# Additive-tanh attention on one Trainium2 core: weighing the 32-row query terms of the next block later in the tanh stretch

## The chip, the cores and the metric

The kernel runs on one core of a Trainium2 chip. The core has a matrix engine (PE, with its weight loads shown as PEld), a vector engine (DVE), a scalar engine for activation functions (ACT), a general engine (POOL) and a queue engine that issues transfers (SP). The metric is the device time of one execution in microseconds (us). The program is launched once and computes the whole model, so the time holds much more than the part that is changed here.

## The reference

The model has an image part (layer 0: projections, a small convolution, a selective scan in four directions) and a token part (layer 1: attention, then a recurrent layer). Only the attention bears on the change. It works on 4 batches of 4096 tokens (64 x 64) with 128 channels, and has 32 hidden units:

```python
t = _to_tokens(x)                                  # 4 x 4096 x 128
t = t + _L1_attn_ref(_ln_t(t), Wt, Wx, bh, Wa, ba)

def _L1_attn_ref(x, Wt, Wx, bh, Wa, ba):
    q = jnp.einsum('bld,ud->blu', x, Wt)           # 32 units for each query
    k = jnp.einsum('bld,ud->blu', x, Wx)           # 32 units for each key
    beta = jnp.tanh(q[:, :, None, :] + k[:, None, :, :] + bh)
    alpha = jnp.einsum('bsju,u->bsj', beta, Wa[:, 0]) + ba[0]
    alpha = jnp.tanh(alpha)
    alpha = jax.nn.softmax(alpha, axis=-1)
    return jnp.einsum('bsj,bjd->bsd', alpha, x)
```

For each pair of a query and a key a sum of 32 weighted tanh terms is formed, then a tanh of that sum, then a softmax over the 4096 keys of a query, and the weights are applied to the normalised tokens. The inner tanh over 4 x 4096 x 4096 x 32 elements is what the kernel avoids.

## The kernel before

Three parts run one after the other: `_layer0`, then the attention `_rational` (from line 1242 on), then the recurrent layer `_chunked`. Only `_rational` changes. Inside it the instructions go to each engine's queue in the order in which the Python program writes them; no scheduler moves them. An instruction waits for the ones it depends on, and everything behind it in the same engine's queue waits with it. Tiles come from pools with a fixed number of buffers, so a new tile also waits until the oldest one has been read.

**The mathematics.** tanh(q + k) is a ratio of expressions in exp(q) and exp(k), and a group of several such terms is one fraction whose numerator and denominator are sums of products of one factor of the query with one factor of the key. The factors of the queries are kept in `E` (128 rows x 2 sides x 512 queries), those of the keys in `F` (128 rows x 2 sides x 4096 keys). A matrix product of some rows of `F` with the same rows of `E` gives the denominators (tile `pd`, function `lower`), and a product with the weighted rows `cE` gives the numerators (tile `pn`, function `upper`). `cE` is `E` times one constant per row, formed by `weigh` (L1379): two DVE instructions, one for each side, of 128 x 512 elements. All products of these two functions have the line L1393 in the profile.

The rows are cut into three units. Unit A uses side 0 in two terms of 64 rows. Units B1 and B2 use side 1, each in two terms of 32 rows. `cE`'s side 0 is read only by `upper` of A, its side 1 only by `upper` of B1 and of B2.

**Blocks and key tiles.** There are 32 blocks: 4 batches, in each 8 blocks of 512 queries. Each block goes over 32 key tiles (`jt`) of 128 keys, and each key tile over the three units. In the steady loop one unit is: two products into `pd` (PE), Ln of it on ACT (L1524), Exp of the negative on ACT (L1527), so that these two form the reciprocal, two multiplications with the numerators on DVE (`times`, L1414), and for B1 and B2 an addition to the sum of unit A on POOL (L1533). `whole` (L1518) on DVE then adds the two halves of the tile's ratio and stores the argument of the outer tanh for 128 keys x 512 queries in `A[:, jt, :]`. In the loop, PE writes the `pd` of a unit two steps ahead and its `pn` one step ahead. The pools have 2 buffers for `pd`, 3 for `pn`, 1 for the product `ct`, 4 and 5 for the ratios `ra` and `rb`, and 1 for `cE`.

Single steps lie between the units of the loop as well, held in the table `between`: the queries of the next block, the transposes of the next batch, the layer norm of the next batch's tokens (`norm_within`, not in the last batch), and the end of the block before (`closing`). Its last step adds the result to the residual tile `xr` on POOL (L1462).

**The block change.** After the last key tile, ACT needs another function table and has the tanh and the exponential of the whole block to do (L1583, L1584), in four parts of 4, 8, 8 and 12 key tiles (`PARTS`). During this stretch, the "tanh stretch", ACT can form no reciprocals, so the next block's first key tile is done by DVE alone, in the function `direct`: for each half of a unit a reciprocal (L1424) and a multiplication with the numerator (L1425). The function `ahead` writes it in four steps, one behind each part of the tanh: step 0 forms the `pd` of A and B1, `upper` of A and `direct` of A; step 1 the `pd` of B2, `upper` and `direct` of B1 and the POOL addition L1574; step 2 the next key tile's `pd` of A, then `upper` and `direct` of B2 and the addition L1578; step 3 another `pd`. Between the steps PE forms `weighted` (L1557), the product of the finished weights with the tokens `xT`, for the parts up to key tile 20; the other 12 key tiles' products lie in the next block's loop. `direct` has an argument `then`, called once behind the first half of its unit; step 0 uses it for the last `whole` of the old block.

Before the change, DVE's order at a block change is therefore: the `times` of the old block's last units, `cE` side 0, `cE` side 1, then for unit A reciprocal, product, `whole`, reciprocal, product, then the same pairs for B1 and B2. PE's order is: the `pd` of A and B1, `upper` A, `weighted` of 0 to 3, the `pd` of B2, `upper` B1, `weighted` of 4 to 11, the `pd` of the next A, `upper` B2, `weighted` of 12 to 19, the `pd` of the next B2, and then the loop.

Where the batch changes (three times: behind blocks 7, 15 and 23) the block is "turned": the factors `F` of all keys of the new batch are formed first (`all_keys`, L1342 to L1351, with 16 maxima on DVE), ahead of step 0 and behind `weigh`.

## Time and profile before

| what | us |
|---|---|
| median of 3 runs | 10629.57 |
| the runs | 10622.62 to 10634.68 |
| profiled execution, its own time | 10622.87 |
| span of the profile in that execution | 10621.1 |
| PE, DVE, ACT, POOL busy, whole span | 9213.9, 9043.7, 9094.5, 8609.3 |
| the same from 3750 to 10400 us, a stretch of 6650 us that is all attention | 6209.2, 5517.2, 6530.7, 5074.8 |
| mean granted clock of PE | 0.942 of full speed |

An execution on one core is profiled by the hardware; the page that is made of it gives the busy time of each engine, the span in 40 slices, and groups of instructions with count, busy time, mean time of one (ns), and the idle time of the engine ahead of them with what ended it. A line such as `x1986 | 2443.0, 1230 | 26.9 <-PE pd L1393 24.6` reads: 1986 instructions, 2443.0 us busy, 1230 ns each; ahead of them the engine stood idle for 26.9 us, of which 24.6 ended when PE had finished a product into `pd` of line 1393. `32*128 32x512 f32` at a product are the rows of its weights and the columns, then the rows and columns of what is moved through. "PEclk" and "granted clock" are the TensorE clock that the throttle granted, as a share of full speed. In the timeline, the first figure is the start in us from the start of the span, the second the time until the last of the group's instructions ended, and in square brackets stands the idle time ahead of it with what ended it. Line numbers are those of the kernel before.

### The profile page before, as it was taken

To read this page: it belongs to the slowest core of one execution; us is meant where nothing else is said; L and a number is where in the kernel's file an instruction comes from. 1 tells how busy PE (TensorE), PEld (TensorE's weight loads), DVE (VectorE), ACT (ScalarE), POOL (GpSimd) and SP (SyncE) were. 2 spreads that over 40 slices of the span, in tenths; PEclk is the share of its full clock that TensorE was granted. 3 is DMA by queue.
4 is the path that set the end of the run, shared out by engine and by line. 5 is a ranking of instruction groups with operands and counts; after the bars stand their busy time and mean duration, and the time that the engine had idled before them with its cause. 6 is when DMAs were issued, how large, how long until landed. Compare 5 with 4: busy or idle time off the path is not lost.

```text
span 10621.1 us, 110120 instructions
## 1 busy us (share of the span) xinstructions
PE 9213.9 (87%) x35452; PEld 3226.5 (30%) x35452; DVE 9043.7 (85%) x10031; ACT 9094.5 (86%) x10279; POOL 8609.3 (81%) x3686
## 2 busy tenths in 40 slices
PE   7787787787777799999999999999999999999997
PEld 2121221222211233333333333333333333333334
DVE  7999999999999788888888888888888888888882
ACT  4566666766766799999999999999999999999995
POOL 7999899999999777788678778877888777767773
PEclk8898898898888999999999999999999999999998
DMA  6889889888888200000000000000000000000001
GB/s 150 200 191 213 189 193 212 194 197 209 198 199 203 71 4 4 4 4 7 4 4 4 7 4 4 7 4 4 4 7 4 4 3 5 3 3 3 5 2 66
DMA packets 228573, 739.50 MB, mean 70 GB/s; under 512 B 41536, under 2 KB 42368, under 8 KB 226448
## 3 DMA queue, kind: packets, MB, share of 16 engines
q1 hardware_dynamic: 224576, 730.76, 29.2%
q8 instruction: 280, 4.59, 0.2%
q14 instruction: 309, 2.53, 0.1%
q10 hardware_dynamic: 3408, 1.63, 0.1%
HBM read 609.15 MB, written 118.88 MB: 69 GB/s over the span
## 4 chain that ended last, share of the span: by engine, by line
PE 35%; ACT 21%; DVE 5%; issue 5%; POOL 1%; DMA 0%; DVEq 0%; POOLq 0%; ACTq 0%; SPq 0%
PE pd L1393 16%; PE pn L1393 10%; PE ct L1557 6%; ACT rb L1527 6%; ACT rb L1524 6%; ACT ra L1524 2%; ACT A L1583 2%; DVE rb L1414 2%; ACT ra L1527 2%; ACT A L1584 1%; DVE ra L1424 1%; PE vy L1758 1%; POOL ra L1533 0%; DVE cE L1379 0%; ACT E L1300 0%
## 5 line engine op out<-in xcount | busy, mean ns | idle before, releaser
L1533 POOL TENSOR_TENSOR ra<-ra,rb 128x1024 f32<-128x1024 f32 x1986 | 5000.9, 2519 | 813.0 <-ACT rb L1527 446.5
L1393 PE MATMUL pn<-cE,F 32*128 32x512 f32 (+1 forms) x12288 | 4602.5, 643 | 88.3 <-DVE rb L1414 78.0
L1393 PE MATMUL pd<-E,F 32*128 32x512 f32 (+1 forms) x12288 | 4037.8, 650 | 342.9 <-ACT ra L1524 239.8
L1414 DVE TENSOR_TENSOR rb<-rb,pn 128x512 f32<-128x512 f32 x3972 | 2543.4, 682 | 582.4 <-PE pn L1393 576.8
L1527 ACT ACTIVATE rb<-rb 128x1024 f32<-128x1024 f32 x1986 | 2513.6, 1270 | 0.0
L1524 ACT ACTIVATE rb<-pd 128x1024 f32<-128x1024 f32 x1986 | 2443.0, 1230 | 26.9 <-PE pd L1393 24.6
L786 POOL TENSOR_TENSOR dBu<-dtdu,bbcc 128x1024 f32<-128x1024 f32 x1024 | 2391.4, 2365 | 88.8 <-DMA dtdu<-dd 58.2
L1393 PEld LDWEIGHTS pd<-E,F 32*128 32x128 f32 (+1 forms) x12288 | 1209.9, 186 | 2257.2 <-ACT ra L1524 972.1
L1393 PEld LDWEIGHTS pn<-cE,F 32*128 32x128 f32 (+1 forms) x12288 | 1420.9, 186 | 1317.3 <-DVE rb L1414 647.0
L1414 DVE TENSOR_TENSOR ra<-ra,pn 128x512 f32<-128x512 f32 x1986 | 1356.1, 686 | 384.8 <-PE pn L1393 287.4
L826 PE MATMUL py<-h,gather 128*32 128x512 f32 x4096 | 1190.6, 677 | 391.7 <-POOL h L812 372.9
L1527 ACT ACTIVATE ra<-ra 128x1024 f32<-128x1024 f32 x993 | 1258.0, 1267 | 0.0
L1524 ACT ACTIVATE ra<-pd 128x1024 f32<-128x1024 f32 x993 | 1210.4, 1219 | 52.6 <-PE pd L1393 43.7
L781 ACT ACTIVATE pa<-dtdu,a_neg 128x1024 f32<-128x1024 f32 x1024 | 1143.6, 1117 | 34.7 <-DMA dtdu<-dd 11.2
L802 DVE TENSOR_TENSOR_SCAN pa<-pa,carry,dBu 128x1024 f32<-128x1024 f32 x480 | 1125.4, 2345 | 32.3 <-ACT pa L781 22.9
L1557 PE MATMUL ct<-A,xT 128*128 128x512 f32 x2048 | 1046.4, 639 | 10.5 <-ACT A L1584 10.5
L812 POOL TENSOR_TENSOR h<-h,bbcc 128x1024 f32<-128x1024 f32 x381 | 899.3, 2360 | 121.8 <-ACT carry L810 104.9
L810 ACT COPY carry<-pa 128x1 f32<-128x1 f32 x643 | 103.0, 160 | 883.9 <-DVE h L809 883.3
L809 DVE TENSOR_TENSOR h<-pa,bbcc 128x1024 f32<-128x1024 f32 x643 | 787.7, 1225 | 61.7 <-PE py L826 1.7
L1518 DVE TENSOR_TENSOR A<-ra 128x512 f32<-128x512 f32 x993 | 753.9, 759 | 35.9 <-POOL ra L1533 31.6
L802 DVE TENSOR_TENSOR_SCAN h<-pa,carry,dBu 128x1024 f32<-128x1024 f32 x288 | 673.2, 2341 | 21.3 <-PE py L826 10.6
L826 PEld LDWEIGHTS py<-h,gather 128*32 128x32 f32 x4096 | 221.8, 116 | 1255.9 <-issue 529.0
(306 smaller groups left out, 8282.2 us busy)
## 6 DMA issues: line engine op xcount, KB each, us to landing
bbcc<-bcd SPq DMA_DIRECT2D x1024, 256.0 KB, 7.7
dtdu<-ddd SPq DMA_DIRECT2D x1008, 256.0 KB, 7.8
ddd<-dd SPq DMA_DIRECT2D x63, 1024.0 KB, 5.1
src<-src SPq DMA_DIRECT2D x60, 512.0 KB, 9.7
xs<-in_x_dram SPq DMA_DIRECT2D x32, 256.0 KB, 7.3
src<-xs SPq DMA_DIRECT2D x16, 512.0 KB, 6.2
bcd<-bc SPq DMA_DIRECT2D x64, 128.0 KB, 1.9
src<-xsT SPq DMA_DIRECT2D x16, 512.0 KB, 5.4
```

Source lines behind the costliest of these rows:

```text
L781: nc.scalar.activation(dA, its[m].DT[r][:, 0, :], AF.Exp, scale=a)
L786: nc.gpsimd.tensor_tensor(dBu, its[m].DT[r][:, 1, :], its[m].BC[q][:, 0, :], ALU.mult)
L802: nc.vector.tensor_tensor_scan(to[:, step], dA[:, step], live.pop(("dBu", u))[:, step], 0.0 if m % nch == 0 else its[m - 1].carry[:, col : ...
L809: nc.vector.tensor_tensor(h, dA, cc, ALU.mult)
L812: nc.gpsimd.tensor_tensor(h, h, cc, ALU.mult)
L826: nc.tensor.matmul(it.y[to, c], gather, live["h", v][:, c], start=False, stop=(q == QS - 1))
L1393: nc.tensor.matmul(ps[a], F[lo:hi, i, jt * P : (jt + 1) * P], side[lo:hi, i, :], start=True, stop=True)
L1414: nc.vector.tensor_tensor(r[:, a, :], r[:, a, :], ns[a], ALU.mult)
L1524: nc.scalar.activation(r, D.pop(i), AF.Ln, scale=LOWER)
L1527: nc.scalar.activation(r, r, AF.Exp, scale=-1.0)
L1533: nc.gpsimd.tensor_tensor(R[at, 0], R[at, 0], R.pop((at, p)), ALU.add)
L1557: nc.tensor.matmul(ct, xT[:, jt, :], A[:, jt, :], start=(jt == 0), stop=(jt == JT - 1))
```

## The change

`weigh` no longer does its two multiplications itself. It makes the tile `cE` and returns it with a function `side(i)` that does one of them. At the kernel's start both sides are still done at once. At each of the 31 block changes side 0 is done where both were done before, and side 1 is done inside `direct` of the next block's unit A: behind the second half's product with the numerator, the place that the argument `then` now names as a pair (behind the first half the old block's last `whole`, as before; behind the second half side 1). The first step that reads side 1 is `upper` of B1, in `ahead(1)`.

DVE's order at a block change becomes: `cE` side 0, reciprocal, product, `whole`, reciprocal, product (unit A), `cE` side 1, then the pairs of B1 and B2. The order on PE, ACT, POOL and SP is as before. The lines behind L1379 move by one to five in the changed kernel.

```diff
--- before.py
+++ after.py
@@ -1375,9 +1375,11 @@
 
     def weigh(E):
         cE = one.tile([P, 2, QB], F32, name="cE")
-        for i in range(2):
+
+        def side(i):
             nc.vector.tensor_scalar(cE[:, i, :], E[:, i, :], c_n[:, i : i + 1], None, ALU.mult)
-        return cE
+
+        return cE, side
 
     groups = {
         "A": (0, ((0, 64), (64, 128))),
@@ -1424,8 +1426,7 @@
             nc.vector.reciprocal(r[:, a, :], d[:, a, :])
             nc.vector.scalar_tensor_tensor(r[:, a, :], r[:, a, :], 1.0 / LOWER, ns[a], ALU.mult, ALU.mult)
             if then is not None:
-                then()
-                then = None
+                then[a]()
         return r
 
     def order(jt):
@@ -1479,7 +1480,9 @@
     for steps in [keys(F, xn, 0, pn, i) for i in range(2)] + [queries(E, xn, 0, i) for i in range(2)]:
         for go in steps:
             go()
-    cE = weigh(E)
+    cE, side = weigh(E)
+    for i in range(2):
+        side(i)
     start = 0
     first = lower("A", F, 0, E), lower("B1", F, 0, E)
     between = {}
@@ -1550,7 +1553,9 @@
             assert not between
 
             if more:
-                E, cE = E_next, weigh(E_next)
+                E = E_next
+                cE, side = weigh(E)
+                side(0)
             ct = pw()
 
             def weighted(jt, ct=ct, xT=xT):
@@ -1567,7 +1572,7 @@
                     return
                 if step == 0:
                     held["A"], held["B1"] = lower("A", F, 0, E), lower("B1", F, 0, E)
-                    held["A"] = direct(held["A"], upper("A", F, 0, cE), "A", lambda: whole(JT - 1))
+                    held["A"] = direct(held["A"], upper("A", F, 0, cE), "A", (lambda: whole(JT - 1), lambda side=side: side(1)))
                 elif step == 1:
                     held["B2"] = lower("B2", F, 0, E)
                     held["B1"] = direct(held["B1"], upper("B1", F, 0, cE), "B1")
```

## Prediction

> **What bounds the kernel now.** I read the page first: from slice 14 on, ACT, PE and DVE are all near full, so the page alone cannot say which one sets the pace of the attention. The stretches of single blocks say it. A block here is the time from one table load of L1583 to the next.

> ```profile
> core 0: us, PE busy (x) PEld busy (x) DVE busy (x) ACT busy (x) POOL busy (x), PEclk, DMA share, GB/s
> 8016.00:8224.00 208.00, 195.69 (x844) 71.22 (x844) 174.85 (x243) 207.15 (x202) 162.02 (x66) 0.98 0.01 5
> 9082.00:9294.00 212.00, 194.66 (x842) 72.14 (x840) 174.09 (x241) 206.22 (x199) 162.49 (x66) 0.97 0.01 3
> ```

> ACT is busy 207.15 of 208.00 us in a short block and hardly less in a long one: ACT paces a block, and a block is long by the time ACT stands idle. Listed by their starts, 15 of the 31 block changes stand before no ACT idle at all (start to start 208.1 us); four wait 0.34 to 0.81 us; nine wait 2.29 to 2.46 us (210.5 to 211.8 us); three, where the batch changes, last 228 us. The waits of ACT over the attention give the whole sum:

> ```profile
> ACT ra L1524 <- PE pd L1393: 43.5, 37, 2.7
> ACT rb L1524 <- PE pd L1393: 24.6, 15, 2.5
> ```

> The second line holds the waits at block changes: 24.6 us is the ceiling of what a shorter change can give. The first line is mostly a stall inside the blocks, which returns below. Next, the timelines of two changes, a clean one (load at 8016.29) and a waiting one (load at 9082.91):

> ```profile
> 8018.58 3.89 DVE L1379 TENSOR_SCALAR cE<-E,consts 128x512 f32<-128x512 f32 x2
> 8022.39 3.35 DVE L1424 RECIPROCAL ra<-pd 128x512 f32<-128x512 f32 x1
> 8023.80 5.13 PE L1557 MATMUL ct<-A,xT 128*128 128x512 f32 x8
> 8030.45 0.70 PE L1393 MATMUL pd<-E,F 32*128 32x512 f32 x2 [1.53 <-DVE ra L1424]
> 8040.70 7.13 PE L1557 MATMUL ct<-A,xT 128*128 128x512 f32 x16
> 8049.00 1.02 ACT L1524 ACTIVATE rb<-pd 128x1024 f32<-128x1024 f32 x1
> ...
> 9088.20 3.70 PE L1557 MATMUL ct<-A,xT 128*128 128x512 f32 x8 [0.40 <-ACT A L1584]
> 9097.11 1.22 PE L1393 MATMUL pd<-E,F 32*128 32x512 f32 x2 [5.21 <-DVE ra L1424]
> 9099.13 8.50 PE L1557 MATMUL ct<-A,xT 128*128 128x512 f32 x16
> 9117.97 1.02 ACT L1524 ACTIVATE rb<-pd 128x1024 f32<-128x1024 f32 x1 [2.33 <-PE pd L1393]
> ```

> The reader should follow one chain: DVE cE, reciprocals of A, the release of pd to PE, then PE without a hole to the pd that ACT's second Ln (L1524) needs. In the second change the same 16 products take 8.50 us instead of 7.13 and the first 32-row product 1.22 instead of 0.70: PE runs at half clock. The granted clock in fine stretches confirms it, 0.50 from 9095.08 to 9101.89; in the clean change the half clock fell earlier, 8016.47 to 8026.70, under the tanh, where nobody waits. All such stretches are multiples of 3.41 us, on one grid.

> **What moves.** Per block change one instruction: cE's side 1 goes from ahead of the first reciprocal to behind the second product of unit A. No DMA, no ACT or PE instruction moves; DVE alone is reordered, and no queue is passed.

> At the old place side 1 is dear, because POOL is still adding: the lone pair at 3611.6 us took 0.48 us each, and behind POOL's last adds the pair takes 3.89 us; of it the second is 2.58 and holds DVE 2.5. At the new place, 12 us after the load, POOL is idle (it stands 17.2 us before L1574), so I take 0.48. DVE's chain gains 2.5 at its head and is 2.0 shorter behind side 1.

> [...]

> Who else waits for side 1? PE's upper of B1, and behind it in PE's order all `weighted` of 4 to 12. In a clean change upper A ends at 8023.9 (half clock), so product A0 can't start before that: 8023.9, 0.6, whole 0.6, reciprocal 3.45, product 0.6, side 1 0.5 gives 8029.6, against 8030.45 for PE's release now. PE finishes its `weighted` at 8028.93. So it comes 0.9 us earlier, not 2.5, for all that follows to 8048.9. ACT does not follow: it had no idle there, and its Tanh, Exp and table load end at 8048.0 whatever PE does. Gain of a clean change: 0.

> The four waits of 0.34 to 0.81 us fall to 0, since 0.9 to 1.7 exceeds them: 3 x 0.81 + 0.34 = 2.8 us. In the nine waiting changes PE ends `weighted` at 9091.9 and the release moves from 9097.1 to 9094.6, with side 1 at 9095.7. The hole shrinks from 5.2 to 2.7, yet the stretch 9091.67 to 9095.06 stays nearly empty, so the half clock still begins at 9095.1. Upper B1 (2.0 at half clock), then 4.1 us of half-rate products and 4.9 at full rate end at 9106.9 instead of 9107.55: a gain of 0.65 of 2.33.

> **What it costs.** PE now reaches the start of the next loop earlier, but its third pd comes free only when ACT has read the first (8048.0 + 1.02). PE's hole before it grows from 0.18 to 1.1 us, in the grid stretch 8047.17 to 8050.58, which held 4.0 (all products weighted by rows, one 128-row pass as 1; a full stretch holds 7.8). The 0.9 us of `weighted` that leaves is 0.9 / 0.441 = 2 passes, so 2.0 to 2.8 stay. Counted over the attention, every stretch followed by half clock held 2.9 or less, and every other one 3.1 or more. So I expect half clock in 8050.6 to 8054.0. There the unit-A products (0.53 a step, 1.0 at half) come 1.6 us late where Ln had 0.35 slack: ACT loses 1.0 to 1.6, say 1.4; two stretches would make 2.1.

> How little a hole need be is seen inside the blocks, where every block has the same 2.15 us hole (POOL's xr add delays whole):

> ```profile
> 8170.96 0.69 PE L1393 MATMUL pn<-cE,F 64*128 64x512 f32 x1 [2.15 <-DVE rb L1414]
> ...
> 9027.70 1.22 PE L1393 MATMUL pn<-cE,F 64*128 64x512 f32 x1 [2.15 <-DVE rb L1414]
> ```

> One hole, two outcomes: a boundary of the grid cuts the first in two. [...]

> **Sum** on the profiled execution (span 10621.1, its own time 10622.87, 6.70 under the median 10629.57):
> - Clean changes: 15 x 1.4, but only for phases where the stretch holds hole and loop start (2.6 of 3.41): +16.
> - Waiting changes: -2.8, and two of the first three batches x 0.65 = -1.3.
> - Last batch: seven blocks of 211.6 us x 0.65 = -4.6, say -5.
> - Batch changes: the first reciprocal there follows the key reductions, so taking side 1 from the front saves nothing; upper B1 now waits for it, one product, side 1: ACT's wait 0.36 becomes 1.7. 3 x 1.3 = +4.
> - The hole inside: blocks now sit at 208.1, close to 61 x 3.41 = 208.2, so the phase stays where the hole is cut. Longer blocks lose that. 0.65 of 3.41 us of phase is safe, so 81% of 23 blocks against 5 now, at 0.5 to 1.9, mean 1.0: 0 to 14, I take half, +7.

> Together +18: 10640.9, and 10648 at the median. A measurement of this kernel tells 0.2% (21 us) from no change.

> **Rivals.**
> [...]
> - *Slower: lasting collision of POOL and DVE.* Place: `whole` (L1518), 2.83 instead of 0.69 when a POOL add starts first. The last full block (load 10141.1) shows it after a half-clock event: waits of 2.1 and 2.7 us more, 216.7 us. Price about 2 us in each block; from half the blocks on it decides: 18 + 16 x 2 = +50, 10680.
> - *It does nothing*: excluded on DVE (2.5 us goes), possible for ACT, which then shows only phase drift, within 9 us.

> **Chances.** Forecast case 0.50 (its parts run from +0 to +35, so 0.28 within 0.2%, 0.22 slower); first rival 0.28 (0.13 within, 0.15 faster); collision 0.19, slower; nothing 0.03. So faster 0.15, same 0.44, slower 0.41. Range: from the cheap end of the first rival, 10608, to past the collision, 10688; its own range for the forecast case is 10630 to 10665.

> **What would show it.** Right: second cE near 0.48 us; PE's hole before `lower` B2 gone in clean changes; granted clock 0.50 about 34 us after a load; ACT idle about 38 us after it; fewer 208.1 blocks. Wrong: block starts still 208.1 apart and L1524's 24.6 us fallen to a few.

## The result

The changed kernel takes 10677.57 us (median of 5 runs, 10666.58 to 10683.64) against 10629.57 us (median of 5, 10622.62 to 10641.11): a ratio of 1.0044 with a 95% interval of 1.0032 to 1.0057, 48 us more. The profiled executions stand 60.7 us apart (spans 10681.8 and 10621.1). Of that, 56 us lie in the 31 blocks from one table load of the tanh to the next (6609.4 us together against 6553.4).

What the change does to DVE is what was forecast. This is a clean change (the half clock of the tanh stretch, 7642.19 to 7652.43 us, falls where nobody waits for it) of the new kernel, with the load at 7641.84 us, from the timelines of DVE, PE and ACT:

```profile
7644.13 1.40 DVE L1380 TENSOR_SCALAR cE<-E,consts 128x512 f32<-128x512 f32 x1
7645.45 3.34 DVE L1426 RECIPROCAL ra<-pd 128x512 f32<-128x512 f32 x1
...
7654.55 0.48 DVE L1380 TENSOR_SCALAR cE<-E,consts 128x512 f32<-128x512 f32 x1
...
7674.63 1.13 PE L1395 MATMUL pd<-E,F 32*128 32x512 f32 x4 [1.12 <-ACT ra L1527]
...
7678.98 1.02 ACT L1527 ACTIVATE ra<-pd 128x1024 f32<-128x1024 f32 x1 [0.68 <-PE pn L1395]
```

Side 1 is done in 0.48 us instead of 2.58. The first reciprocal starts 3.61 us after the load, 2.5 us earlier than before. PE comes early to the loop and stands for 1.12 us there. Then follows the half clock (0.50 from 7676.35 us), and ACT waits 0.68 us. The stretch with PE's hole, the stretch of the half clock behind it, and the two kinds of block that the new kernel has most of, by windows:

```profile
core 0: us, PE busy (x) PEld busy (x) DVE busy (x) ACT busy (x) POOL busy (x), PEclk, DMA share, GB/s
7672.93:7676.35 3.42, 2.30 (x12) 0.72 (x10) 0.69 (x1) 3.41 (x5) 0.83 (x1) 1.00 0.00 0
7676.35:7679.75 3.40, 3.40 (x12) 0.98 (x12) 1.38 (x2) 2.72 (x4) 0.00 (x0) 0.50 0.02 5
...
7641.84:7850.72 208.88, 197.63 (x845) 71.16 (x845) 173.13 (x243) 207.35 (x201) 162.56 (x66) 0.97 0.01 4
...
4437.56:4649.18 211.62, 196.96 (x845) 71.72 (x845) 172.88 (x243) 207.46 (x201) 161.79 (x66) 0.98 0.01 4
```

ACT's work is the same in both (207.4 us), so a block is long by what ACT waits, as before. But no block of the new kernel lasts 208.1 us, where 13 did; twelve of the 31 last 211.5 to 211.8 us, where six did. 211.63 us are 62 stretches of the clock's grid (62 x 3.4133; 945 such stretches lie between the starts of the new kernel's half clocks at 4450.73 and 7676.32 us). Ten blocks of the first two batches stand on that value one behind the other (1 to 6 and 11 to 14, counted by their table loads from 0). ACT's waits over the attention:

```profile
ACT ra L1527 <- PE pd L1395: 62.4, 54, 2.7
ACT rb L1527 <- PE pd L1395: 41.7, 22, 3.2
ACT E L1300 <- DVE top L1297: 18.9, 8, 2.4
```

The first was 43.5 and the second 24.6; the third, the exponentials of the next queries waiting for DVE, is not among the first five of before. Sorted by their place in the block (my sums over the rows of ACT's timeline), the waits at the loop start rose by 18 us (26.2 to 44.6), those at and just behind the stall inside the block by 25 us (44.6 to 70.0), the others in the loop by 11 us, and those in the tanh stretch fell by 3.5 us. These sums mix two opposite movements. The 21 ordinary blocks of the first three batches lost 44 of the 56 us: there the waits at the loop start rose by 22 us (7.6 to 29.9), and those at the stall, 120 us further on, by 13 us (17.8 to 31.0). In the seven blocks of the last batch, which lost 7 us, the waits at the loop start fell by 11 us and those at the stall by 6 us, while 17 us of waits that the kernel before did not have came just behind the stall.

**Why ten blocks hold at 62 stretches.** Call a block's phase the time from the last line of the 3.41 us grid to its table load. At phase 0.48 the new kernel's block runs like this (the block from 4437.56 us, from the timelines of PE and ACT and by windows): the half clock from 4450.73 to 4457.55 makes ACT wait 2.01 us at the loop start; the hole inside the block then lies almost wholly in the stretch from 4590.67 to 4594.08, and the next stretch has the half clock too.

```profile
4449.24 1.13 PE L1395 MATMUL pd<-E,F 32*128 32x512 f32 x4 [2.68 <-DVE ra L1426]
...
4472.31 1.02 ACT L1527 ACTIVATE rb<-pd 128x1024 f32<-128x1024 f32 x1 [2.01 <-PE pd L1395]
```

```profile
4450.73:4457.55 6.82, 6.82 (x11) 2.27 (x8) 6.72 (x3) 6.79 (x3) 0.00 (x0) 0.50 0.00 0
4590.67:4594.08 3.41, 1.49 (x8) 0.55 (x4) 3.25 (x2) 3.41 (x6) 2.44 (x2) 1.00 0.53 154
4594.09:4597.50 3.41, 3.19 (x12) 1.02 (x12) 2.04 (x4) 1.82 (x4) 2.35 (x1) 0.50 0.00 0
```

The columns of the windows are as above; the clock is the third from the end. ACT's timeline behind the hole:

```profile
4596.45 1.02 ACT L1527 ACTIVATE ra<-pd 128x1024 f32<-128x1024 f32 x1 [1.59 <-PE pd L1395]
```

The wait of 1.59 us stands where the clean block from 7641.84 us has 0.66 (at 7798.48). With 0.37 more behind it, the block comes to 211.62 us, and the next one starts at the same phase.

The order of before meets the same phase in one block of a run shown below (e7, load at 8028.71 us, phase 0.43; this batch's code is that of before). Its wait at the loop start is longer, 2.83 us, and so its hole ends 157.52 us after the load instead of 156.75. A line of the grid cuts it in two, and the clock stays full (windows, then ACT's timeline at the loop start and behind the hole):

```profile
8028.71:8239.65 210.94, 193.80 (x845) 70.99 (x845) 174.87 (x243) 207.26 (x201) 162.05 (x66) 0.98 0.01 5
8041.94:8048.76 6.82, 5.88 (x13) 2.32 (x14) 6.61 (x5) 6.79 (x3) 0.00 (x0) 0.50 0.00 0
8181.89:8185.30 3.41, 2.18 (x12) 0.59 (x4) 2.55 (x1) 3.41 (x6) 3.13 (x2) 1.00 0.44 152
8185.30:8188.71 3.41, 2.48 (x15) 0.94 (x18) 2.89 (x6) 2.75 (x5) 1.77 (x1) 1.00 0.01 5
```

```profile
8064.28 1.02 ACT L1530 ACTIVATE rb<-pd 128x1024 f32<-128x1024 f32 x1 [2.83 <-PE pd L1394]
...
8187.43 1.02 ACT L1530 ACTIVATE ra<-pd 128x1024 f32<-128x1024 f32 x1 [0.66 <-PE pd L1394]
```

210.94 us is 0.69 short of 62 stretches, so the phase moves back by 0.69 us, and the next block lasts 208.10 us. So the shorter wait of the new order is the dearer one. This rests on one block of the old order; blocks of e5, with a little more work on ACT, wait 2.8 us at the same phases and also keep the full clock behind the hole (e5, 4436.76 us: a wait of 2.82 us, then 1.00 in the three stretches from 4590.4 to 4600.6).

### The profile page after: what moved, and what is told of

Same layout as the page of the kernel before. It is cut to its first block, busy times and chain, and to the rows that moved or that the text cites. A ratio compares the mean times of both kernels' runs of the same rounds, so it can differ in the third digit from the quotient of the medians.

```text
span 10681.8 us, 110120 instructions
## 1 busy us (share of the span) xinstructions
PE 9252.4 (87%) x35452; PEld 3232.9 (30%) x35452; DVE 9006.2 (84%) x10031; ACT 9099.9 (85%) x10279; POOL 8605.3 (81%) x3686
## 4 chain that ended last, share of the span: by engine, by line
PE 38%; ACT 18%; DVE 5%; issue 4%; POOL 1%; DMA 0%; DVEq 0%; ACTq 0%; SPq 0%; POOLq 0%
PE pd L1395 17%; PE pn L1395 11%; PE ct L1562 7%; ACT rb L1530 6%; ACT rb L1527 5%; ACT ra L1527 2%; DVE rb L1416 2%; ACT ra L1530 2%; ACT A L1588 1%; DVE ra L1426 1%; ACT A L1589 1%; PE vy L1763 1%; POOL ra L1536 1%; DVE A L1521 0%; ACT E L1300 0%
## 5 line engine op out<-in xcount | busy, mean ns | idle before, releaser
L1521 DVE TENSOR_TENSOR A<-ra 128x512 f32<-128x512 f32 x993 | 779.0, 785 | 39.7 <-POOL ra L1536 35.1
```

## The experiments

The first four ran with the theory that PE's early arrival is the cause. A new order that is dear by itself would be dear in any kernel; so most of the later ones put the same edit into both orders.

**e1: side 1 at both places.** Behind `side(0)`, ahead of `ct = pw()`:

```diff
                 side(0)
+                side(1)
```

> The changed kernel with side 1 weighed at both places: at the old place again (ahead of the first reciprocal, beside POOL's additions) and, a second time with the same values, at the new one. Theory (PE comes early): the change costs time because DVE starts its reciprocals 2.5 us earlier, PE follows 0.9 us earlier and finds a hole ahead of the loop's products, whose half clock pushes the blocks out of the harmless phase. With the front paid again, PE's times are those of before and the late side 1 adds at most 0.5 us to a chain with cover: 10630 to 10645 us, most blocks 208.1 us again, no half clock 34 us after a load. Rival (side 1 is too late for upper of B1): the late place is still there, so the time stays that of the changed kernel, 10670 to 10685.

Measured: 10712.36 us (ratio 1.0079, 1.0066 to 1.0093), slower than either kernel; neither text holds. DVE's front is as long as before, so the reciprocals are not earlier, and the late side 1 is now felt:

```profile
4241.08 1.13 PE L1395 MATMUL pd<-E,F 32*128 32x512 f32 x4 [1.53 <-DVE ra L1426]
4242.27 1.13 PE L1395 MATMUL pn<-cE,F 32*128 32x512 f32 x4
```

In the order of before the denominators of B2 and the numerators of B1 run through PE side by side (from 8030.45 and 8030.47 us in the change above from 8016.29); here the second start only when side 1 is there (4242.22), and everything behind them is 1.17 us later. ACT waits 1.16 us at the loop start of these otherwise clean changes, and 83 us there in all. So the late place costs 1.2 us where the front is not shortened: the rival's mechanism exists, but the change pays it out of the 2.5 us that it saves.

**e2 and e8: two products and one product with zero weights on PE.**

```diff
                     for jt in range(lo, hi):
                         weighted(jt)
+                    if more and i == 0:
+                        for _ in range(2):      # e8: range(1)
+                            nc.tensor.matmul(ct, zero, A[:, 0, :], start=False, stop=False)
```

> The changed kernel with two products with zero weights (128 rows, 512 columns, 0.44 us each at full clock) added to ct on PE behind the first part's weighted products, ahead of the pd of B2: they fill 0.9 us of the place where PE stood before. Theory (PE comes early): in clean changes PE arrives at the loop as late as before, the hole of 1.1 us and the half clock at 34 us go, the blocks are 208.1 us again and keep their phase: 10615 to 10645 us. Rival (side 1 is too late): PE gets only more work, 10675 us or more. Third (the lock at 211.6 us, whatever the loop start): waiting changes keep their half clock at 13 us, and most blocks of the first two batches still last 211.6: 10665 to 10680.

> The changed kernel with one product with zero weights (0.86 us of PE in two passes, as the run with two of them showed) behind the first part's weighted products, so that PE reaches the loop as late as in the kernel before. Theory (PE comes early, then the phase): clean blocks of 208.1 us, no half clock at 34 us, the phase kept over many blocks in the first three batches; the time is near before, 10630 to 10660, most of what is left in the last batch and the three changes of batch. Rival (lock at 211.6 us in the first two batches all the same): 10665 to 10680.

Measured: 10667.40 us with two (1.0037, 1.0024 to 1.0051), 10676.98 with one (1.0038, 1.0024 to 1.0052). A product takes 0.86 us in two passes, so two of them delay PE by 1.8 us, not 0.9 (e2, PE's timeline, and the window of a clean block):

```profile
4656.35 1.88 PE L1604 MATMUL ct<-A,zero 128*128 128x512 f32 x4
```

```profile
4643.88:4852.15 208.27, 197.46 (x849) 72.19 (x850) 172.82 (x243) 207.34 (x201) 162.02 (x66) 0.98 0.01 4
```

With two, twelve blocks last 208.24 to 208.30 us, without a half clock at the loop start: PE's early arrival is indeed what brought it on in the clean changes. But the time fell by some 10 us only; the changes of batch (694 us for the three blocks against 689) and other phases took the rest. With one, the hole of 1.12 us became 0.92 and was still followed by half clock in three blocks (10, 14 and 18; in block 10, 0.50 from 5969.70 us), and eleven blocks lasted 211.6 to 211.8 us: the lock at 211.6 us, of which e2's third text and e8's rival speak, is what e8 shows, and its time lies in their range. The time of e2 lies in that range too, but none of its blocks of the first three batches lasts 211.6 us. So the half clock at the loop start alone is not the 48 us.

**e3 and e4: the addition to xr on DVE, in the new order and in the old.**

```diff
-            nc.gpsimd.tensor_tensor(xr, xr, held["rec"], ALU.add)
+            nc.vector.tensor_tensor(xr, xr, held["rec"], ALU.add)
```

> The changed kernel with the addition to the residual tile xr (the last step of closing) on DVE instead of POOL, for 0.7 us on DVE. Theory: POOL's addition makes the whole beside it last 2.83 us and gives PE the 2.15 us hole inside each block; ACT waits 70 us there in this kernel against 45 in the one before. Without it the hole and its half clock go: 50 to 75 us less than the changed kernel, 10603 to 10628. Rival (DVE is the bound there): the addition on DVE costs as much as it saves, 10665 to 10690.

> The kernel before the change with the addition to xr on DVE instead of POOL. Theory: ACT's 45 us of waits inside the blocks go, 10580 to 10600 us; and the changed kernel with the same edit is 5 to 30 us above it, so that the waits inside the blocks carry about half of what the change costs. Rival (the change's cost lies at the block change alone): the distance between the two stays 45 to 50 us.

Measured: 10676.54 us (1.0046, 1.0033 to 1.0060) and 10696.68 us (1.0063, 1.0050 to 1.0077). The edit does not take the hole away. DVE's addition starts at 7581.12 us, while POOL adds from 7579.98 for 2.73 us, and lasts 2.14 us, where the `whole` at 7579.80 takes 0.69; ACT waits 1.43 us behind it (e4, timelines of DVE and ACT):

```profile
7581.12 2.14 DVE L1462 TENSOR_TENSOR xr<-xr,rec 128x512 f32<-128x512 f32 x1
...
7585.11 1.02 ACT L1524 ACTIVATE ra<-pd 128x1024 f32<-128x1024 f32 x1 [1.43 <-PE pd L1393]
```

The expected gain failed (e3's time lies in its rival's range, e4's in neither), but the pair tells more than it was made for: with another hole at another place, the new order is 20 us **faster** than the old one, and the runs of the two do not overlap. The old order now has 211.7 or 211.8 us in twelve of the 21 ordinary blocks of the first three batches, at phases of 1.5 to 1.8; its waits at the loop start are 51 us against 31. The same edit of the order is worth +48 or -20 us. That fits a cost set by where the blocks come to stand on the grid, and not one that the order has by itself.

**e5 and e6: 0.3 us more of ACT in each block.** In the loop, behind the two activations:

```diff
+                if i == 30:
+                    nc.scalar.activation(junk[:, 0:256], b_a.to_broadcast([P, 256]), AF.Exp)
```

> The kernel before the change with one more ACT instruction in each block (an exponential of 256 columns into a scratch tile, about 0.3 us, in the eleventh key tile, where ACT sets the pace). New theory (phase): a clean block of 208.1 us is almost 61 grid stretches of 3.413 us (208.2), so the kernel before keeps a phase in which the half clock falls under the tanh; 0.3 us more make it drift by 0.2 us a block out of that phase into the waiting changes. Then a sum of 32 x 0.3 = 10 us costs 30 to 70 us, 10660 to 10700, and fewer than ten blocks are under 209 us. Rival (only what the instruction itself takes): 10635 to 10648.

> The changed kernel with the same 0.3 us ACT instruction in each block. Phase theory: the changed order itself waits less (about 1.9 us at a waiting change against 2.4, over a narrower stretch of phases); only its clean blocks no longer keep their phase. When both kernels drift, the changed one is not the slower one: 10650 to 10690, from 0 to 30 us under the kernel before with the same instruction. Rival (the new order costs its 45 us wherever the phase is): 10685 to 10735, 45 us above the other.

Measured: 10653.39 us (1.0014, 1.0005 to 1.0023) and 10673.91 us (1.0037, 1.0023 to 1.0051). The instruction lengthens a clean block by 0.38 us (208.10 to 208.48), 12 us in all. The old order pays 18 us, 6 more than the instruction itself: its phase drifts up as was expected, but at 0.43 to 0.50 a block waits 2.8 us once and is thrown back, so blocks of 208.5 and 211.3 alternate:

```profile
4436.76:4648.07 211.31, 194.13 (x845) 71.05 (x845) 175.08 (x243) 207.64 (x202) 161.93 (x66) 0.98 0.01 4
4648.07:4856.59 208.52, 196.10 (x845) 71.39 (x846) 174.99 (x243) 207.65 (x202) 162.23 (x66) 0.98 0.01 5
```

The new order pays nothing (10673.91 against 10677.57): the fixed point at 0.48 is gone with it. No block of the first two batches is held there, and one of the third meets that phase (load at 8263.39 us, 212.5 us) and leaves it again; in the last batch five blocks are held at 211.62 us, at phase 1.35. Between the two lie 20 us instead of 48 (of the 26 us between their 31 blocks in the profiled executions, 15 lie in the three changes of batch). My 30 to 70 us for the old order were too many, and its time lies in neither range; the new order's time lies in its range, but it did not come out level with the old one or below it.

**e7: the last batch's ACT work filled up.** In the blocks without `norm_within`:

```diff
+            else:
+                for at in ((16, 2), (22, 1), (22, 2)):
+                    between.setdefault(at, []).append(
+                        lambda: nc.scalar.activation(junk, b_a.to_broadcast([P, QB]), AF.Exp))
```

> The kernel before the change with three more ACT instructions in each block of the last batch (512 columns each, about 0.55 us, at the places where the other batches have the three of the layer norm), into a scratch tile. Phase theory: the last batch's blocks are held at 211.6 us (62 grid stretches) because without the norm's ACT work they are too short for 61 and wait; with 1.7 us more work each, they reach the phase of the other batches and last 208 to 209.5: the work of 13 us that is added takes 15 to 30 us away, 10600 to 10617. Rival (the waits there are not a matter of phase): 10640 to 10650.

Measured: 10638.67 us (1.0001, 0.9992 to 1.0010). The gain did not come; the time is 1 us under the rival's range. The last batch's blocks still lasted 211.67 us, now at phases of 2.2 to 2.3, with waits of 1.64, 0.7 and 1.8 us: another sum that makes 62 stretches.

**e9 and e10: the addition to xr on DVE from PSUM.** The `times` on DVE have one operand in PSUM; all 5958 of them last 0.63 to 0.69 us in the kernel before, though POOL is busy for 162 of a block's 208 us. So the addition gets an operand in PSUM too:

```diff
-            nc.vector.tensor_tensor(held["rec"], held["rec"], held["num"], ALU.mult)
-            nc.gpsimd.tensor_tensor(xr, xr, held["rec"], ALU.add)
+            nc.vector.tensor_tensor(held["num"], held["rec"], held["num"], ALU.mult)
+            nc.vector.tensor_tensor(xr, xr, held["num"], ALU.add)
```

> The kernel before the change with the end of closing done on DVE alone and in another way: the product of rec and num goes back into num's PSUM tile, and DVE adds that to xr (0.7 us, an operand in PSUM, which the runs show beside POOL's additions at no loss), so that neither POOL's extra addition nor DVE's wait for POOL (2.14 us in the run with the plain addition on DVE) is left. Theory (the hole inside the block is half of the matter): ACT's 45 us of waits inside the blocks fall below 15, a clean block lasts 207.4 us, the phase drifts by 0.8 us a block, waits at the loop start stay at 20 to 45 us: 10590 to 10620. Rival (DVE's extra 0.7 us comes through to ACT): 10630 to 10660.

> The changed kernel with the same edit. Theory: the changed order costs time only by the way its phase meets the hole inside the block (a waiting change of 2.0 us and a half clock after the hole make 211.62 us, 62 grid stretches, a fixed point); without that hole no block is held at 211.6 us, and the change moves the time by no more than 15 us either way against the other kernel with this edit: 10590 to 10625. Rival (the changed order costs its 45 us at the block change itself): 10635 to 10665, 45 us above the other.

Measured: 10616.32 us (0.9987, 0.9978 to 0.9996) for the old order and 10618.16 (0.9991, 0.9982 to 1.0000) for the new one. Both theories hold in the time: without the hole inside the block the change costs 2 us, not 48. The edit also shortens a clean block by 0.5 to 0.7 us and so moves both orders off their old phases. A shift alone (e5 and e6) left 20 us; that another shift, with the hole kept, would have left none is not excluded. DVE's addition and PE's stall behind it in e10, by the timeline, and ACT's waits:

```profile
4584.34 0.69 DVE L1463 TENSOR_TENSOR xr<-xr,ct 128x512 f32<-128x512 f32 x1
...
4585.68 0.69 PE L1395 MATMUL pn<-cE,F 64*128 64x512 f32 x1 [0.41 <-DVE rb L1416]
```

```profile
ACT rb L1527 <- PE pd L1395: 33.1, 19, 2.0
ACT ra L1527 <- PE pd L1395: 16.8, 14, 2.7
```

PE's stall is 0.41 us instead of 2.15. In the first three batches no wait is left there; a clean block lasts 207.4 to 207.6 us, and one or two clean blocks and a waiting one of 209.1 to 209.3 us follow each other in both orders. What is left of the second line comes from the last batch, where POOL and DVE still meet; five blocks of e10 there still last 211.6 to 211.8 us.

**e11 and e12: the edits of e9 and e7 together**, in both orders.

> The kernel before the change with the addition to xr from PSUM on DVE and with the three extra ACT instructions in each block of the last batch. With the hole inside the block gone, the last batch's seven full blocks (1493 us together in the run with the PSUM addition alone) are held up by POOL and DVE meeting, because ACT is 1.7 us a block faster there than in the other batches; with the same ACT work they should go as those do, 208.4 us on average, the last full one about 214: 1464 us, 29 less, 10587 to 10605. Rival (those waits come from POOL's own pace, not ACT's): 13 us of work added for nothing, 10620 to 10635.

> The changed kernel with the same two edits. The last batch's blocks (1487 us in the run with the PSUM addition alone) should come to 1464 too, 10590 to 10605; and if the change costs only by its phase at the hole inside the block, it stays within 15 us of the other kernel with these edits. Rival as there: 10620 to 10635.

Measured: 10587.22 us (0.9960, 0.9946 to 0.9973) and 10586.86 us (0.9957, 0.9944 to 0.9971), the fastest of all, 0.4% under the kernel before: at the low end of what was expected for the old order, 3 us below it for the new one. The ACT work that was added in the last batch now takes about 30 us away: its blocks 24 to 30 come to 1456 us in e12 against 1487 in e10. And the two orders are equal within 1 us. Two blocks in a row of e12:

```profile
4218.94:4426.31 207.37, 194.87 (x845) 70.75 (x845) 171.40 (x244) 207.18 (x202) 161.27 (x65) 0.98 0.01 5
4426.31:4635.42 209.11, 194.61 (x845) 71.21 (x845) 171.50 (x244) 207.28 (x202) 161.01 (x65) 0.98 0.01 5
```

Here the parts of the change can be read with the least beside them, by one execution of each. In the ordinary blocks of the first three batches the new order lasts 208.22 us on average against 208.32, 2 us less over 21 blocks; the three changes of batch last 688.0 us against 681.6, 6 us more.

## Why the prediction was right, and where its sum was not

The time forecast was 10648 us with a range of 10608 to 10688; measured are 10677.57 us. The sign of the likeliest case is right and the range holds the result, but the sum is short: +18 forecast, +48 measured (56 between the blocks of the profiled executions).

- *The chain on DVE and PE*: right. Side 1 takes 0.48 us. In a waiting change PE's product of B2 starts 11.7 us after the load instead of 14.2, and the hole ahead of it is 2.68 us instead of 5.2 (2.7 forecast). In a clean change PE's products behind side 1 start 14.3 us after the load instead of 15.2, the 0.9 us of the forecast; PE's hole at the loop start is 1.12 us (1.1 forecast), and the half clock follows it 34.5 us after the load. What the hole inside the block suggested holds at the loop start too: the window at 7676.35 shows 0.50 behind a hole of 1.12 us.
- *Clean changes, 15 x 1.4 for 2.6 of 3.41 phases = +16*: this is the step that failed. Where the half clock came 34 us after the load, ACT lost 0.67 to 0.89 us there, half of the forecast, and only four blocks had it (10, 18, 22 and 30), because a block that is 0.7 us longer leaves that phase at once. The term took the changes to stay of the kind that they were. In the first three batches 14 of the 21 ordinary changes are now waiting ones, with the half clock 12 to 13 us after the load and 1.7 to 2.0 us of wait, where there had been two. The waits at the loop start rose by 22 us there; the +12 of this term and the next is not far off, but by another way.
- *Waiting changes, -0.65 each*: right in size. The wait fell from 2.3 or 2.5 us to 1.7 or 2.0. But nine such changes became sixteen. Of the four short waits that were to fall to 0, two went and two stayed (0.58 and 0.33 us).
- *Batch changes, +4*: right in sum, in part by luck. The three blocks lasted 1.24, 1.12 and 1.99 us longer, together 4.4. Their waits at the loop start came to 3.2 us each, not 1.7, and so rose by 7.4 us; 3.6 us of other waits in the tanh stretch went.
- *Last batch, -5*: wrong. Its seven blocks took 7 us more; the shorter waits at the loop start (-11) and at the stall (-6) were given back at new meetings of POOL and DVE behind it.
- *The hole inside the block, "23 blocks against 5 now, mean 1.0: 0 to 14, I take half, +7"*: too small, and by the same step. In the 23 blocks of which it speaks the waits at the stall rose by 12 us (20.1 to 32.3). I took the phases as spread evenly and independent of the waits. They are not: each block's length sets the next one's phase, and a length of 62 stretches repeats itself. The lengths that the new order has at phase 0.48 make such a point, the old order's at the same phase (210.94) does not. Blocks 1 to 6 and 11 to 14 alone carry 33 of the 56 us; each has 2.0 us more than a clean block of before at the loop start and 1.3 us more at the stall.
- *The first rival's 0.28, and the range from 10608*: they stand for a loop start without half clock. No run shows a length of hole below which the half clock stays away: it followed a hole of 1.12 us (after, 7676.35) and, in three blocks of e8, one of 0.92 us. What parted the stretches was the count by rows, at 3.0 to 3.1.
- *The rival of lasting collisions, 10680*: near in time, and in part in cause. Every block has one long `whole` at the stall; 15 more stand in the new kernel's block 10 and in the seven blocks of the last batch, where before had two. This is one in block 25, from the timelines of DVE and ACT, with the exponential of the next queries that waits behind it:

```profile
9296.84 2.83 DVE L1521 TENSOR_TENSOR A<-ra 128x512 f32<-128x512 f32 x1 [0.31 <-POOL ra L1536]
...
9300.30 0.60 ACT L1300 ACTIVATE E<-ct 128x512 f32<-128x512 f32 x1 [2.37 <-DVE top L1297]
```

  ACT's waits behind such additions rose by about 28 us (17 just behind the stall, 11 elsewhere in the loop). But the last batch gave 17 us of it back in shorter waits, and the collisions came in 8 of 31 blocks, not in half of them.
- *Why before is fast*: the prediction had the remark that 208.1 is close to 61 stretches, and gave it 7 us. What it was worth to the kernel before is less than I came to think: leaving that length by 0.38 us a block cost 6 us beyond the instruction itself. The new order paid nothing for the same 12 us of work, because it left the length of 62 stretches by it.
- *Readings*: of the fifteen changes without a wait, two (blocks 9 and 22) stand in blocks of 210.0 us, not 208.1; of the nine waiting ones, the last stands in the block of 216.7 us. The median of before less all of the 24.6 us is 10605, and the range starts at 10608.

Not settled: which phase a run enters the attention with (the blocks of one kernel differ a little from run to run, 17 us between the changed kernel's fastest and slowest). In e8 a hole of 0.92 us brought the half clock in blocks 10, 14 and 18 and not in 11, 12 and 19. The prediction's count by rows tells them apart: the stretch with the hole held 2.8, 2.9 and 2.9 there, and 3.2, 3.1 and 3.4 here. That the fixed point is left when the hole is removed is shown for the first three batches; the lengths as a function of the phase were read from the blocks that occurred, not measured phase by phase.

## What to carry to other kernels

## What was not expected of the hardware

- The half clock followed stalls and made stalls (0.50 from 4594.09 us behind a hole of 2.14 us, then ACT's wait of 1.59 us), and the two together held blocks at a whole number of 3.41 us stretches: lengths of 211.6 us (62 x 3.413) came about by different sums of waits, in the kernel before (last batch), the changed one, e1, e4, e6, e7, e8 and e10 (last batch).
- A hole of 2.15 us in PE's work was followed by half clock or not, by where the grid cut it: 1.49 us of work in the stretch before gave 0.50, 2.18 and 2.48 us on both sides of the line gave 1.00. PE's busy time alone did not tell: the stretch from 7672.93 was busy for 2.30 us and gave 0.50. Counted by rows as in the prediction (a 128-row pass is 1, spread over its duration), these held 2.0 and 2.6 ahead of 0.50, and 3.4 and 4.2 ahead of 1.00; over the attention of both kernels the two kinds part at 3.0 to 3.1.
- A DVE addition of two tiles in SBUF lasted 2.14 us (e4, 7581.12) and 2.83 us (`whole`, 9296.84) beside POOL's additions, against 0.69 us as the median of all 993 `whole` (before, L1518); the addition to xr with one operand in PSUM lasted 0.69 us (e10, 4584.34). No run shows by what DVE is held up.
